# Where the attention mask of a fused state-space and attention kernel is applied: in the score matmuls, or, for the last of four groups, as products with the exponentials

## The chip, the cores and the metric

The kernel runs on one core of one Trainium2 chip. A core has five engines that run side by side, each with its own queue in program order: TensorE (PE in the profile; its weight loads are a row of their own, PEld), VectorE (DVE), ScalarE (ACT), GpSimd (POOL) and SyncE (SP), which here issues most of the DMAs. The metric is the device time of one execution in microseconds (us); lower is better.

## What is computed

The input is 32 sequences of 256 tokens with 256 channels. Each goes through a state-space layer (a projection, a short convolution, a layer norm, a recurrence over the tokens, a gate and an output projection) and then through two transformer layers with local attention and a feed-forward part; the input is added to the result. The part that matters here is the attention:

```python
# 8 heads of 64, windows of 128 tokens; each window looks at itself and at the one before
sim = jnp.einsum('bhwid,bhwjd->bhwij', bq, bk)
mask = (i < j) | (i > j + WINDOW) | (j == -1)
sim = jnp.where(mask, -jnp.finfo(sim.dtype).max, sim)
attn = jax.nn.softmax(sim, axis=-1)
out = jnp.einsum('bhwij,bhwjd->bhwid', attn, bv)
```

A query sees no later token, and of the window before only the tokens up to 128 back.

## The kernel before, in words

The 32 sequences are worked on in four groups of eight. The state-space part of a group is a scan over its 256 time steps, all eight sequences together (`group_scan`): VectorE does one recurrence step a token (L703), ScalarE scales the input rows (L693), TensorE reads the states out (L715), and SP loads the rows (L672). The scan of group 0 runs alone at the start. After that the scan of group g+1 runs beside the attention and feed-forward work of group g; when the last group has its turn, there is no scan left to run beside it.

The transformer work is a list of 64 turns, `seqs`: four groups, two layers, eight sequences. Each turn's work is cut into steps, and `stage(n, i, ...)` puts a step of turn n into stage i of eight (i may run on into the stages of later turns); a loop over the stages then emits the steps, in the order in which they were put into the list. So the attention of turn n stands beside the feed-forward steps of turns n-1 to n-3 and the projections of turn n+1. The order of the calls is the program's order; a scheduler may still move instructions within an engine's queue, unless `tc.keep_in_program_order` holds an instruction where it was written.

The steps of one turn that the change touches or that stand beside it:

- `project` (L962) projects queries, keys and values of the next turn, on TensorE, in stages 0, 1, 3 and 4; `rotated` then squares on ScalarE (L975), multiplies on VectorE (L978, L983), sums on VectorE (L988, L992), and on GpSimd adds (L986), takes a power (L994) and multiplies (L995).
- `turn` (L1001) transposes queries and keys on TensorE; ScalarE copies them (L1006).
- `scores(b, kw, i0, n)`: keys of window kw (0 or 1), pairs of heads i0 to i0+n. For each of two banks of PSUM, one matmul of the 128x128 identity (bf16) with the mask (bf16, repeated over the heads, 512 columns) writes the mask into the bank (L1161); the score matmuls (L1168) then add the scores to it. ScalarE takes the exponential of the whole bank into `pT` (L1177). The mask holds 0 where a key is seen and -32768 where not, so that the exponential there is 0. Scores of kw=1 stand in stage 2, of kw=0 in stages 3 (pairs 0 and 1) and 5 (pairs 2 and 3).
- `sums` (L1187) and `values` (L1206), both in stage 7, read `pT` on TensorE: the sums of the exponentials by head, and their products with the values. The reciprocal of the sums (L1195) goes through DRAM and comes back spread over the partitions; `divide` (L1230, VectorE, stage 4 of the next turn) multiplies it in, and `finish` (L1012 on TensorE, L1020 on VectorE, stage 6 of the next turn) does the output projection and adds it to the residual `res`.
- The feed-forward part: `normalise` (L1248, L1252 to L1258), `apply` (L1265), `spread` (L1278, L1280), `widen` (L1301 on TensorE, L1309 on ScalarE), `product` (L1317 on VectorE), `narrow` (L1329 on TensorE, L1340 on VectorE). In layer 1 `narrow` also adds the kernel's input on GpSimd (L1348) and issues the output's DMA.

All tiles in PSUM come from one pool of eight banks, and `pT` has six buffers, which is what one turn needs.

The tile of the mask is made once, at the set-up:

```python
mask_t = const.tile([P, 2 * W], BF, tag="mask_t", name="mask_t")
nc.gpsimd.memset(mask_t, 0.0)
nc.gpsimd.affine_select(
    out=mask_t[:, 0:W], in_=mask_t[:, 0:W], compare_op=ALU.is_ge, fill=MASKED_LOW,
    base=0, pattern=[[1, W]], channel_multiplier=-1,
)
```

The second half of it is filled in the same way with the sign turned round. The program holds a second path, `exact`, for inputs with large scales; it is not taken with these inputs and is the same in both kernels.

Of the kernel before, what the change touches and what calls it, by code (L numbers as in the profile page):

```python
# [11 lines left out]
BF = mybir.dt.bfloat16  # L12
I32 = mybir.dt.int32
AF = mybir.ActivationFunctionType
ALU = mybir.AluOpType
# [4 lines left out]
P = 128  # L20
# [18 lines left out]
W = 128  # L39
# [13 lines left out]
def bc(ap, axis, n):  # L53

    ap = ap.unsqueeze(axis)
    shape = list(ap.shape)
    shape[axis] = n
    return ap.broadcast_to(shape)
# [15 lines left out]
def kernel(  # L74
# [29 lines left out]
    nc = tc.nc  # L104
    B = xT.shape[2]
    L = wqkv.shape[1]
    NG = B // GB

    const = ctx.enter_context(tc.tile_pool(name="const", bufs=1))
# [53 lines left out]
    for j in range(NJ):  # L163
# [13 lines left out]
    mask_t = const.tile([P, 2 * W], BF, tag="mask_t", name="mask_t")  # L177
    ident_b = const.tile([P, P], BF, tag="ident_b", name="ident_b")
# [7 lines left out]
        out=mask_t[:, W : 2 * W], in_=mask_t[:, W : 2 * W], compare_op=ALU.is_ge,  # L186
        fill=MASKED_LOW, base=0, pattern=[[-1, W]], channel_multiplier=1,
    )

    head_cols = const.tile([P, 2, 32], FP, tag="head_cols", name="head_cols")  # L190
    nc.gpsimd.memset(head_cols, 0.0)
# [27 lines left out]
    def program(ctx, exact):  # L219
# [802 lines left out]
        if exact:  # L1022

            mask = rpool.tile([P, 2 * W], FP, tag="mask", name="mask")
# [102 lines left out]
        class Attention:  # L1127

            def __init__(self, l):
                self.l = l
                self.qkv, self.rot, self.p, self.o = {}, {}, {}, {}

            def project(self, b, w, a):
                if w == 0 and a == 2:
# [16 lines left out]
            def scores(self, b, kw, i0, n):  # L1153


                qT, kT, _ = self.qkv[b]
                nq = S - kw * W
                banks = []
                for r in range(2):
                    sc = ps_w.tile([P, n, nq], FP, tag="w", name="sc")  # L1160
                    nc.tensor.matmul(  # L1161
                        sc, ident_b, bc(mask_t[:, 0:nq], 1, n), start=True, stop=False
                    )
                    banks.append(sc)
                for i in range(n):
                    for r in range(2):
                        rows = slice(r * DH, (r + 1) * DH)
                        nc.tensor.matmul(  # L1168
                            banks[r][:, i, :],
                            kT[rows, i0 + i, kw * W : (kw + 1) * W],  # L1170
                            qT[rows, i0 + i, kw * W :],
                            start=False,
                            stop=(i == n - 1),
                        )
                for r in range(2):
                    p = aw.tile([P, n, nq], FP, tag="pT", name="pT", bufs=6)
                    nc.scalar.activation(p, banks[r], AF.Exp)  # L1177
                    for i in range(n):
                        self.p[b, kw, i0 + i, r] = p[:, i, :]

            def sums(self, b):

                rs = bank(ps_w, "w", "rs")[:, 0:S]
                for kw in range(NW):
                    for r in range(2):
                        for i in range(HEADS // 2):
                            nc.tensor.matmul(  # L1187
                                rs[32 * i : 32 * i + 32, kw * W :],
                                head_cols[:, r],
                                self.p[b, kw, i, r],  # L1190
                                start=(kw == 0 and r == 0),
                                stop=(kw == NW - 1 and r == 1),
                            )
                rinv = aw.tile([P, S], FP, tag="rinv", name="rinv", bufs=1)
                nc.vector.reciprocal(rinv, rs)  # L1195
                self.rinv = rinv
# [183 lines left out]
        seqs = [(g, l, b) for g in range(NG) for l in range(L) for b in range(GB)]  # L1380
        stages = {}

        def stage(n, i, what, *args):
            stages.setdefault(ST * n + i, []).append(partial(what, *args))

        def attend(n, at, b, nxt):

            stage(n, 0, at.turn, b, 1)
            stage(n, 3, at.scores, b, 0, 0, 2)
            stage(n, 2, at.scores, b, 1, 0, HEADS // 2)  # L1390
            stage(n, 5, at.scores, b, 0, 2, 2)
            stage(n, 7, at.sums, b)
            stage(n, 7, at.values, b)
            stage(n + 1, 0, at.put_inverse)
            stage(n + 1, 2, at.load_inverse)
            stage(n + 1, 4, at.divide, b)
            stage(n + 1, 6, at.finish, b)
            if nxt is not None:
                for w in range(NW):
                    for i, a in ((0, 2), (1, 0), (1, 1)):  # L1400
                        stage(n, 3 * w + i, nxt[0].project, nxt[1], w, a)
                stage(n, 6, nxt[0].turn, nxt[1], 0)
# [23 lines left out]
            if l == L - 1 and g < NG - 1:  # L1426
                stage(n + 6, 2, load_res, g + 1, b)

        ats = [Attention(l) for _, l, _ in seqs]

        for n, (g, l, b) in enumerate(seqs):
            nxt = (ats[n + 1], seqs[n + 1][2]) if n + 1 < len(seqs) else None
            attend(n, ats[n], b, nxt)
            feed(n, g, l, b)
# [24 lines left out]
        for t in range(max(stages) + 1):  # L1459
# [3 lines left out]
            g, r = divmod(t + 1 + group - reload, group)  # L1463
# [10 lines left out]
    with tc.If(fits > 0) as which:  # L1474
        with ExitStack() as es:
            program(es, False)
    with which.Else():
        with ExitStack() as es:
            program(es, True)
# [81 lines left out]
def _program(ins, out_shape):  # L1561
    import concourse.bacc as _bacc

    nc = _bacc.Bacc("TRN2", target_bir_lowering=False, num_devices=1)
    arrays, args = {}, []
    for name, a in ins.items():
        arrays[f"in_{name}_dram"] = a
        args.append(
            nc.dram_tensor(
                f"in_{name}_dram", a.shape, mybir.dt.from_np(a.dtype), kind="ExternalInput"  # L1570
            ).ap()
        )
    args.append(nc.dram_tensor("out_0_dram", out_shape, FP, kind="ExternalOutput").ap())
    with tile.TileContext(nc) as tc:
        kernel(tc, *args)
    return nc, arrays
# [11 lines left out]
```

## Time and profile before

| What | us |
|---|---|
| median of three runs (3755.57 to 3771.47) | 3759.6 |
| the profiled execution | 3750.8 |
| its span in the profile | 3748.7 |
| scan of group 0 alone, before the first score matmuls | 0 to 528 |
| one turn of the last group | 41.6 |
| last score matmuls of the last turn | about 3680 |

The profile's page gives, for each engine, its busy time, and then the span in 40 slices with the busy share in tenths. "Chain of waits" is the chain of work that ended last, followed back from the end. A timeline line gives the start, the duration, the engine, the line of the kernel, the operation, output and input tiles, shape and count; what stands in brackets at its end is the time for which the engine had been idle and what ended that. In a run of several instructions merged into one line ("x8") the duration runs from the first start to the last end, so that two lines of TensorE overlap a little. TensorE's float32 matmuls stand in the trace as two instructions each.

### The profile page before, as it was taken

The numbers are of one execution on the slowest core, as the hardware profiler recorded it, in microseconds if no ns is written. First come the engines' busy times: TensorE is split into PE (matmuls) and PEld (weight loads), VectorE is DVE, ScalarE is ACT, GpSimd is POOL, SyncE is SP. The second block draws the span as 40 slices with busy tenths as digits, with TensorE's granted clock in tenths as the row PEclk, the third lists the DMA queues.
The fourth block names the chain that finished last, engine by engine and source line by source line (L and its number), as shares of the span: only waits on it lengthen the run. The fifth ranks groups of instructions, "written<-read, shape, count | busy, mean of one in ns | idle before, by whom it ended". The sixth has DMA issues, their size and how long they took to land.

```text
span 3748.7 us, 57254 instructions
## 1 busy us (share of the span) xinstructions
PE 3601.1 (96%) x19900; PEld 2242.4 (60%) x19900; DVE 2669.6 (71%) x5177; ACT 2195.4 (59%) x3817; POOL 1834.9 (49%) x1776
## 2 busy tenths in 40 slices
PE   7999889999999999999999999999999999999998
PEld 4444335656656665665666665656666666666666
DVE  6888889888787787778777877777777444444443
ACT  4666656666666666666666665666666444444442
POOL 4433466545555565455455555645444444434441
PEclk9999999999999999999999999999999999999999
DMA  7777655445454545434444545444443211011101
GB/s 210 205 198 202 189 163 149 120 117 135 127 137 129 147 123 146 120 112 122 120 128 116 147 124 147 121 108 126 112 129 103 57 40 50 12 34 34 30 25 35
DMA packets 469214, 435.81 MB, mean 116 GB/s; under 512 B 228835, under 2 KB 308532, under 8 KB 468788
## 3 DMA queue, kind: packets, MB, share of 16 engines
q1 hardware_dynamic: 384466, 420.05, 40.1%
q10 hardware_dynamic: 84450, 12.01, 2.0%
q8 instruction: 160, 2.62, 0.3%
q14 instruction: 138, 1.13, 0.1%
HBM read 383.70 MB, written 46.66 MB: 115 GB/s over the span
## 4 chain that ended last, share of the span: by engine, by line
PE 62%; DVE 16%; POOL 7%; ACT 6%; DMA 5%; issue 3%; SPq 0%; ACTq 0%; DVEq 0%; POOLq 0%
PE ps_qkv L962 12%; PE pa L1301 12%; PE po_f L1329 7%; DVE h L703 6%; PE y L715 4%; PE ps_wo L1012 4%; DMA xrep<-xnd 4%; PE sc L1168 4%; PE ov L1206 3%; PE ps_out L793 2%; ACT xrep L693 2%; DVE acc L485 2%; PE tr_qk L1001 2%; PE ps_in L395 2%; POOL acc L474 2%
## 5 line engine op out<-in xcount | busy, mean ns | idle before, releaser
L703 DVE CUSTOM_DVE_ANT_0 h<-h,xrep,lim 128x512 f32<-128x512 f32 x1024 | 948.2, 926 | 269.2 <-ACT xrep L693 238.8
L693 ACT ACTIVATE xrep<-xrep,beta 128x512 f32<-128x512 f32 x960 | 674.1, 719 | 333.0 <-DMA xrep<-xnd 235.9
L962 PE MATMUL ps_qkv<-qkv,res 128*128 128x512 f32 x1536 | 727.1, 610 | 45.2 <-DVE ag L1317 30.1
L1301 PE MATMUL pa<-hT,w 128*128 128x256 f32 (+1 forms) x3072 | 688.3, 386 | 0.3 <-ACT oT L1213 0.3
L1301 PEld LDWEIGHTS pa<-hT,w 128*128 128x128 f32 (+1 forms) x3072 | 492.9, 178 | 183.7 <-issue 66.5
L962 PEld LDWEIGHTS ps_qkv<-qkv,res 128*128 128x128 f32 x1536 | 282.4, 194 | 335.4 <-issue 263.3
L986 POOL TENSOR_TENSOR rot<-rot,swp 128x512 f32<-128x512 f32 x256 | 336.5, 1314 | 293.0 <-DVE swp L983 239.2
L1258 POOL TENSOR_TENSOR rstd<-ve,neg_half 128x1 f32<-128x1 f32 x128 | 82.7, 646 | 792.9 <-DVE ve L1256 787.8
L994 POOL TENSOR_TENSOR rn<-ss,neg_half 128x8 f32<-128x8 f32 x256 | 460.3, 1798 | 14.8 <-DVE ss L992 5.0
L1329 PE MATMUL po_f<-ag,w 128*128 128x256 f32 (+1 forms) x1536 | 387.8, 394 | 4.8 <-DVE res L1340 1.1
L715 PE MATMUL y<-h,ly 128*32 128x512 f32 x2048 | 354.9, 612 | 12.9 <-DVE h L703 11.7
L1329 PEld LDWEIGHTS po_f<-ag,w 128*128 128x128 f32 (+1 forms) x1536 | 273.6, 190 | 112.9 <-issue 44.6
L1317 DVE SCALAR_TENSOR_TENSOR ag<-pa,b_sb,ag 128x256 f32<-128x256 f32 (+1 forms) x448 | 212.4, 474 | 166.5 <-ACT ag L1309 163.0
L975 ACT ACTIVATE sq<-ps_qkv 128x512 f32<-128x512 f32 x256 | 152.1, 596 | 270.5 <-PE ps_qkv L962 234.6
L995 POOL TENSOR_TENSOR rot<-rot,rn 128x512 f32<-128x512 f32 x256 | 298.6, 1166 | 20.1
L1309 ACT ACTIVATE ag<-pa,b_sb 128x256 f32<-128x256 f32 x320 | 150.4, 470 | 198.5 <-PE pa L1301 197.4
L1012 PE MATMUL ps_wo<-oT,wo 128*128 128x256 f32 x1024 | 231.6, 379 | 0.0
L485 DVE SCALAR_TENSOR_TENSOR acc<-xr,wc_sb,acc 128x256 f32<-128x256 f32 x384 | 192.7, 525 | 52.9 <-POOL acc L474 52.6
L1177 ACT ACTIVATE pT<-sc 128x512 f32<-128x512 f32 x384 | 208.5, 596 | 32.2 <-PE sc L1168 30.7
L1168 PE MATMUL sc<-qT,kT 64*128 64x128 f32 (+1 forms) x2048 | 221.5, 345 | 0.0
L978 DVE TENSOR_TENSOR rot<-ps_qkv,rc_sb 128x512 f32<-128x512 f32 x256 | 175.0, 683 | 56.5 <-ACT sq L975 55.9
L1012 PEld LDWEIGHTS ps_wo<-oT,wo 128*128 128x128 f32 x1024 | 194.5, 190 | 27.2 <-PE y L715 0.8
(150 smaller groups left out, 5534.7 us busy)
## 6 DMA issues: line engine op xcount, KB each, us to landing
xrep<-xnd SPq DMA_DIRECT2D x960, 256.0 KB
rb<-inv SPq DMA_DIRECT2D x128, 256.0 KB
xnd<-xn SPq DMA_DIRECT2D x64, 256.0 KB
qkv<-in_wqkv_dram SPq DMA_DIRECT2D x24, 512.0 KB
ahead<-xs_a SPq DMA_DIRECT2D x48, 256.0 KB
xp<-ahead SPq DMA_DIRECT2D x48, 256.0 KB
xd<-xnd SPq DMA_DIRECT2D x192, 64.0 KB
w<-in_w_dram SPq DMA_DIRECT2D x80, 128.0 KB
```

Of the source, the lines that this page charges most:

```text
L485: nc.vector.scalar_tensor_tensor(acc, xr[:, :, k : k + CH], wc_sb[:, ch, k : k + 1], acc, ALU.mult, ALU.add,)
L693: scaled = nc.scalar.activation(bx, ck[c].pop(("bx", t), bx), AF.Copy, scale=ck[c]["beta"][:, t : t + 1])
L703: nc.vector._custom_dve(TENSOR_ADD_SAT, out=h_new, in0=state["h"], in1=bx, s0=ck[c]["lim"][:, 0, t : t + 1], s1=ck[c]["lim"][:, 1, t : t + 1],
L715: nc.tensor.matmul(ck[c]["y", hb][32 * q : 32 * q + 32, :], ly[hb % 2][:, 32 * t : 32 * t + 32], ck[c].pop(("h", hb * TB + t)), start=(i = ...
L962: nc.tensor.matmul(ps, res[b][:, k, t0 : t0 + W], wt["qkv", a][:, k], start=(k == 0), stop=(k == KM - 1),)
L986: nc.gpsimd.tensor_add(rot, rot, swp)
L994: nc.gpsimd.tensor_tensor(rn, ss, neg_half, ALU.pow)
L995: nc.gpsimd.tensor_mul(rot, rot, bc(rn, 2, DH))
L1012: nc.tensor.matmul(po[:, d], wt["wo", 0][:, c, d * P : (d + 1) * P], oT[:, c, :], start=(c == 0), stop=(c == NC_ - 1),)
L1168: nc.tensor.matmul(banks[r][:, i, :], kT[rows, i0 + i, kw * W : (kw + 1) * W], qT[rows, i0 + i, kw * W :], start=False, stop=(i == n - 1),)
L1301: nc.tensor.matmul(pg if x else pa, wt["w1", m][:, k, x], self.h[:, k], start=(k == 0), stop=(k == KM - 1),)
L1329: nc.tensor.matmul(self.po[:, d], wt["w2", 0][r0 : r0 + n, m, d * P : (d + 1) * P], self.ag[m][r0 : r0 + n], start=(m == 0), stop=(m == le ...
```

## The change

For the last group (`apart`, true for g = NG - 1), `scores` leaves out the matmul that writes the mask, and each score matmul opens and closes its own accumulation. Instead a new step, `mask`, multiplies the exponentials in place by a tile of ones and zeros, `mask_1`, repeated over the heads. It does so on GpSimd for kw=1 (step in stage 3) and on VectorE for kw=0 (steps in stages 4 and 6), two products a step. `mask_1` is made once at the set-up from `mask_t`. The other three groups keep the matmul.

```diff
+    mask_1 = const.tile([P, 2 * W], BF, tag="mask_1", name="mask_1")
+    nc.gpsimd.tensor_scalar(mask_1, mask_t, -1.0, None, ALU.is_ge)
...
-            def __init__(self, l):
+            def __init__(self, g, l):
                 self.l = l
-                self.qkv, self.rot, self.p, self.o = {}, {}, {}, {}
+                self.apart = g == NG - 1
+                self.qkv, self.rot, self.p, self.ps, self.o = {}, {}, {}, {}, {}
...
                     sc = ps_w.tile([P, n, nq], FP, tag="w", name="sc")
-                    nc.tensor.matmul(
-                        sc, ident_b, bc(mask_t[:, 0:nq], 1, n), start=True, stop=False
-                    )
+                    if not self.apart:
+                        nc.tensor.matmul(
+                            sc, ident_b, bc(mask_t[:, 0:nq], 1, n), start=True, stop=False
+                        )
...
-                            start=False,
-                            stop=(i == n - 1),
+                            start=self.apart,
+                            stop=self.apart or i == n - 1,
...
                     nc.scalar.activation(p, banks[r], AF.Exp)
+                    self.ps[kw, i0, r] = p
...
+            def mask(self, kw, i0):
+
+                e = nc.gpsimd if kw else nc.vector
+                for r in range(2):
+                    p = self.ps.pop((kw, i0, r))
+                    n, nq = p.shape[1:]
+                    tc.keep_in_program_order(
+                        e.tensor_mul(p, p, bc(mask_1[:, 0:nq], 1, n))
+                    )
...
             stage(n, 5, at.scores, b, 0, 2, 2)
+            if at.apart:
+                for i, what in ((3, (1, 0)), (4, (0, 0)), (6, (0, 2))):
+                    stage(n, i, at.mask, *what)
             stage(n, 7, at.sums, b)
             stage(n, 7, at.values, b)
...
-        ats = [Attention(l) for _, l, _ in seqs]
+        ats = [Attention(g, l) for g, l, _ in seqs]
```

Beyond the added and removed instructions, the order in which the instructions of group 0's scan stand in the queues of all engines differs in places; those of groups 1 and 2 stand as before.

## The prediction

> **What bounds the kernel now.** I read the page's busy times first, then the slices, then the busy times by stretch, because the change touches one group of four.
>
> ```profile
> PE 3601.1 (96%) x19900; PEld 2242.4 (60%) x19900; DVE 2669.6 (71%) x5177; ACT 2195.4 (59%) x3817; POOL 1834.9 (49%) x1776
> ...
> PE   7999889999999999999999999999999999999998
> ...
> DVE  6888889888787787778777877777777444444443
> ```
>
> ```profile
> 3400.00:3500.00 100.00, 100.00 (x608) 68.25 (x606) 42.02 (x89) 46.74 (x77) 38.68 (x33) 1.00 0.18 47
> 3500.00:3600.00 100.00, 100.00 (x557) 66.06 (x554) 45.12 (x99) 48.07 (x78) 47.10 (x38) 1.00 0.09 22
> ```
>
> In the last quarter (columns of the second fence: length, then busy time of PE, PEld, DVE, ACT, POOL, the clock, DMA share) no scan runs any more: DVE falls to 4 tenths, POOL to 38 to 47%, and PE is busy for all of it at full clock. Of PE's few waits from 2850 us on, the sum is 3.5 us. So in this stage TensorE sets the pace, and a piece of its time taken out shortens the run, as long as nothing else makes it wait. The mask matmuls in that stretch wait for nothing either (120 of them from 2850 us on; the last group's 96 are among these):
>
> ```profile
> L1161 PE MATMUL sc<-mask_t,ident_b x120: 379/379/379, 2871.9 to 3678.9; 128*128 128x512 bf16 x120
> ```
>
> The 379 ns are a latency, not a price. The price is read where PE stands back to back, from the chain of waits and the PE timeline of one sequence:
>
> ```profile
> 3520.74 1.73 PE pa L1301 x8
> 3522.47 0.43 PE sc L1161 x2
> 3522.90 1.06 PE sc L1168 x8
> ```
>
> ```profile
> 3522.31 0.59 PE L1161 MATMUL sc<-mask_t,ident_b 128*128 128x512 bf16 x2
> 3522.83 1.13 PE L1168 MATMUL sc<-qT,kT 64*128 64x256 f32 x8
> ...
> 3529.18 1.04 PE L1001 MATMUL tr_qk<-ident,rot 128*128 128x128 f32 x8
> 3530.05 1.89 PE L1301 MATMUL pa<-hT,w 128*128 128x256 f32 x8
> 3531.88 1.51 PE L1187 MATMUL rs<-pT,head_cols 128*32 128x256 f32 x32
> ```
>
> By ends, a pair of mask matmuls takes 0.43 us; by starts, 0.52 us (3522.31 to 3522.83). A sequence of the last group takes 41.57 us (tp_h starts at 3496.33 and 3537.90) and holds three pairs.
>
> [...] L1168 uses 64 rows, L1161 all 128; the first weight load of L1168 indeed begins only with its first matmul. [...] The trace has 1.22 us for L1230 (1024 columns[...]) and 0.68 for L978 (512)[...]. [...] The trace shows who pays: L1348 takes 1.26 us alone and 2.12 beside L1230, while L1230 stays at 1.21 to 1.22.
>
> **The change part by part.** Sixteen sequences (two layers by eight) belong to the last group.
>
> *Removed.* 16 x 6 = 96 mask matmuls with their weight loads, 48 pairs. At 0.43 us a pair this is 20.6 us, all on the path. Ends of the unknown: 48 x 0.52 = 25.0 us if the start distance were the price; if the 0.19 us load of the first f32 weights of L1168 had so far been hidden by the masks, 48 x 0.24 = 11.5 us. I take 20.6, since the extra 0.09 of the start distance only reflects that a bf16 weight load is shorter[...]. Apart from the masks, the order of PE's instructions in the last group is the same in both programs, so nothing else moves there. That each score matmul now opens its own accumulation costs nothing: the count is the same.
>
> *Added on VectorE.* 64 products of 128x512, four a sequence, between 0.60 us (start distance of L978 and L983) and 0.69 us. Bound [...]above by 1.22 (as if it were 1024 columns). I take 0.65, 2.6 us a sequence on an engine with over 20 us idle.
> The first pair (heads block 0) stands behind L1230:
>
> ```profile
> 3515.83 1.22 DVE L1230 TENSOR_TENSOR oT<-oT,rb 128x1024 f32<-128x1024 f32 x1
> 3517.86 0.48 DVE L1317 SCALAR_TENSOR_TENSOR ag<-pa,b_sb,ag 128x256 f32<-128x256 f32 x1 [0.81 <-ACT ag L1309]
> ...
> 3529.38 0.69 DVE L1020 TENSOR_TENSOR res<-res,ps_wo 128x512 f32<-128x512 f32 x1 [1.70 <-PE ps_wo L1012]
> 3532.49 0.48 DVE L1317 SCALAR_TENSOR_TENSOR ag<-pa,b_sb,ag 128x256 f32<-128x256 f32 x1 [2.42 <-ACT ag L1309]
> ```
>
> It fills the 0.81 us gap and pushes L1317 by 0.5 us; the next operation, L978, waits until 3519.75 for ScalarE, and this ag is read by narrow a sequence later. Cost zero. The second pair is the one that matters: it stands behind L1020, which waits for ps_wo, and sums (L1187) waits for it. L1020 ends at 3530.07; two products take it to 3531.4. sums begins at 3531.88, reads the first product's output as its third head (0.18 us later) and the second's 0.54 us after its start, at 3532.4. Cover left: 1.0 us, and the first product has 1.3. Behind a waiting sums, PE would hold the values, widen and everything after. In the last sequence no turn stands between; L1020 ends at 3686.48, the pair at 3687.8, needed at 3687.95: still no wait.
>
> *Added on GpSimd.* 32 products, two a sequence, 1.04 (L995) to 1.27 us (L986), 2.3 us a pair. [...] In the queue they stand between the first and the second rotation:
>
> ```profile
> 3511.97 1.04 POOL L995 TENSOR_TENSOR rot<-rot,rn 128x512 f32<-128x512 f32 x1
> 3516.04 2.12 POOL L1348 TENSOR_TENSOR fo<-fo,xs 128x512 f32<-128x512 f32 x1 [3.02 <-DVE fo L1340]
> 3521.25 1.27 POOL L986 TENSOR_TENSOR rot<-rot,swp 128x512 f32<-128x512 f32 x1 [3.09 <-DVE swp L983]
> ```
>
> They need the exponentials that ScalarE finished at 3508.0, run in the 3.02 us gap, and end near 3515.3, sixteen us ahead of sums. L1348, which the VectorE pair now also slows, may end 1.2 us later, and so its output DMA; the square L975 that reuses the buffer may then slip by about a us. ScalarE and VectorE have over 1 us idle behind it before the second product. Cost zero.
>
> *Added once.* mask_1, one tensor_scalar of 128x256 on GpSimd in the set-up: 0.56 us by L474, inside the 1.08 us for which GpSimd waits at 3.6 us.
>
> *Moved.* The order of instructions on every engine changes in the first 500 us (group 0's scan), not in groups 1 and 2. On ScalarE the first tanh goes ahead of the last two parameter loads, which now hold it up:
>
> ```profile
> 20.50 0.72 ACT L493 ACTIVATE th<-acc 128x256 f32<-128x256 f32 x2 [9.86 <-DMA b_sb<-in_b_dram]
> ```
>
> SP issues the 768 KB w2 load about a hundred DMAs later, behind the first xq and xrep rows. Both should let the first scan step start 1 to 3 us sooner. In the later chunks single read-out, normalise and copy steps swap places; no duration tells what that costs. I bound the whole by -5 and +12 us (eight chunks by 1.5 us, about the length of two steps) and take -2.
>
> *Sum.* 20.6 + 2 = 22.6 us. The profiled execution took 3750.8 us around a span of 3748.7; it becomes 3728.2. The median of the runs shown is 3759.6, 8.8 above it; the same 22.6 us gives **3737.0 us**, 0.6% less.
>
> **The rivals.** (a) *The first group gives it back.* The re-ordering hits a stage that is bound by VectorE's chain of steps (432 of 527 us busy), where each lost us counts. For: the changes reach all eight chunks. Against: they are swaps of neighbours, and the start looks earlier. With +12 us: 3759.6 - 20.6 + 12 = 3751. (b) *Less is saved than the pair's length*, because the masks hid weight loads[...]: 11.5 us plus the 2 of the start, 3746. For: the first load of L1168 begins late. Against: it began no earlier behind the masks. (c) *The wait at sums takes over, and the kernel is slower.* Place: the second VectorE pair between L1020 and L1187. A pair has 2.35 us (3530.07 to 3532.4) and takes 1.3. Each us beyond is lost 16 times; the gain of 1.29 us a sequence is gone when the pair takes 3.65 us, 1.8 us a product. At 2.5 us a product it loses 2.65 us a sequence: 3759.6 - 22.6 + 42 = 3779. For: TensorE is in order and the cover short. Against: in this stage no VectorE operation of up to 512 columns takes over 0.7 us, except the reciprocal (1.76). That the masks stay on TensorE is excluded: the built order has 288 of 384 left.
>
> **How the numbers follow.** Forecast 0.60, own range 3728 to 3744; (a) 0.17, (b) 0.12, (c) 0.11. About 0.5% (18.8 us) is what a measurement can tell from no change: faster means under 3740.8. Of the forecast 0.55 lies there, of (a) and (b) 0.03 together; within 0.5%: 0.05 + 0.26 = 0.31; slower 0.11. The range, 3728 to 3756, takes in the forecast's ends, (b) and most of (a), and leaves out (c) and the tails.
>
> **What would show it.** Right: 24 mask matmuls from 2850 us on, PE still 100% busy from 3000 to 3600, 40.3 us a sequence, no PE wait for the products at L1187, products at 0.6 to 0.7 us (VectorE) and 1.0 to 1.3 us (GpSimd), first attention projection about 2 us sooner. Wrong: sums waiting for VectorE by over 0.3 us a sequence; scores L1168 taking over 1.2 us in the chain of waits; the first 500 us longer by more than 5.

## The result, and the profile after

| What, in us | before | after |
|---|---|---|
| median of five runs each | 3760.6 (3755.6 to 3771.5) | 3738.0 (3732.7 to 3741.3) |
| the profiled execution | 3750.8 | 3732.7 |
| its span in the profile | 3748.7 | 3730.9 |
| one turn of the last group | 41.57 | 40.28 |
| first residual addition (turn 0) | 597.3 | 595.0 |
| residual additions, turn 0 to turn 46 | 2433.2 | 2438.7 |
| residual additions, turn 46 to turn 63 | 681.5 | 660.8 |

The ratio of after to before is 0.9938, 95% interval 0.9923 to 0.9953: faster by 0.6%, or 22.6 us by the medians. The last three rows cut the profiled executions at the starts of the residual additions (L1020 before, L1023 after; lines move down by 3 to 17), one in each turn. The whole gain lies in the last row, 20.7 us. The row above it moves the other way by 5.4 us; the experiments show what that is worth.

The page of the changed kernel, its busy row and its slices:

```profile
PE 3587.1 (96%) x19804; PEld 2234.2 (60%) x19804; DVE 2719.1 (73%) x5241; ACT 2195.6 (59%) x3817; POOL 1872.6 (50%) x1809
...
PE   7999989999999999999999999999999999999998
...
DVE  6888889888887877787777777777777545555553
```

Busy time by stretch (the columns as before), and the mask matmuls that are left from 2850 us on:

```profile
3400.00:3500.00 100.00, 100.00 (x587) 66.74 (x580) 51.99 (x111) 49.50 (x82) 45.13 (x39) 1.00 0.17 42
3500.00:3600.00 100.00, 100.00 (x550) 68.75 (x548) 55.20 (x108) 48.68 (x77) 56.61 (x45) 1.00 0.09 25
```

```profile
L1167 PE MATMUL sc<-mask_t,ident_b x24: 379/379/379, 2875.1 to 3026.8; 128*128 128x512 bf16 x24
```

PE still has no idle time in the last quarter, with 24 masks in place of 120: the work became less and the bound stayed. DVE went from 42 and 45 to 52 and 55%. The chain of waits shows that nothing came in the masks' place; the feed-forward projection goes straight over into the scores, which take 1.06 us as before:

```profile
3508.81 1.73 PE pa L1318 x8
3510.54 1.06 PE sc L1174 x8
```

The timelines of VectorE, GpSimd and TensorE for one turn of layer 1:

```profile
3503.90 1.36 DVE L1247 TENSOR_TENSOR oT<-oT,rb 128x1024 f32<-128x1024 f32 x1
3505.18 2.35 DVE L1195 TENSOR_TENSOR pT<-pT,mask 128x512 f32<-128x512 f32 x2
3507.45 0.47 DVE L1334 SCALAR_TENSOR_TENSOR ag<-pa,b_sb,ag 128x256 f32<-128x256 f32 x1
...
3517.02 0.69 DVE L1023 TENSOR_TENSOR res<-res,ps_wo 128x512 f32<-128x512 f32 x1 [1.26 <-PE ps_wo L1015]
3517.62 1.29 DVE L1195 TENSOR_TENSOR pT<-pT,mask 128x512 f32<-128x512 f32 x2
```

```profile
3500.90 1.04 POOL L998 TENSOR_TENSOR rot<-rot,rn 128x512 f32<-128x512 f32 x1
3501.90 2.27 POOL L1195 TENSOR_TENSOR pT<-pT,mask 128x512 f32<-128x512 f32 x2
3504.13 2.25 POOL L1365 TENSOR_TENSOR fo<-fo,xs 128x512 f32<-128x512 f32 x1
3509.33 1.28 POOL L989 TENSOR_TENSOR rot<-rot,swp 128x512 f32<-128x512 f32 x1 [2.95 <-DVE swp L986]
```

```profile
3516.82 1.04 PE L1004 MATMUL tr_qk<-ident,rot 128*128 128x128 f32 x8
3517.69 1.89 PE L1318 MATMUL pa<-hT,w 128*128 128x256 f32 x8
3519.51 1.51 PE L1204 MATMUL rs<-pT,head_cols 128*32 128x256 f32 x32
```

The second pair ends at 3518.91, before sums (L1204) begins at 3519.51, and sums takes 1.51 us, as long as before the change. The first pair takes 2.35 us instead of 1.29, next to L1365 on GpSimd; that is so in eight of the 16 turns, in those where L1365 runs beside it. All products together (durations are shortest, median and longest):

```profile
L1195 DVE TENSOR_TENSOR pT<-pT,mask x64: 677/684/1759, 3062.1 to 3669.5; 128x512 f32<-128x512 f32 x64
L1195 POOL TENSOR_TENSOR pT<-pT,mask x32: 1150/1157/1164, 3058.9 to 3653.6; 128x512 f32<-128x512 f32 x32
```

### The profile page after: what moved, and what is told of

It is laid out like the page before. It is cut to its first block, busy times and chain, and to the rows that moved or that the text cites. A ratio compares the mean times of both kernels' runs of the same rounds, so it can differ in the third digit from the quotient of the medians.

```text
span 3730.9 us, 57179 instructions
## 1 busy us (share of the span) xinstructions
PE 3587.1 (96%) x19804; PEld 2234.2 (60%) x19804; DVE 2719.1 (73%) x5241; ACT 2195.6 (59%) x3817; POOL 1872.6 (50%) x1809
## 4 chain that ended last, share of the span: by engine, by line
PE 63%; DVE 16%; POOL 6%; DMA 6%; ACT 5%; issue 3%; SPq 0%; ACTq 0%; DVEq 0%; POOLq 0%
PE ps_qkv L965 13%; PE pa L1318 12%; PE po_f L1346 7%; DVE h L706 6%; PE ps_wo L1015 5%; PE y L718 4%; PE sc L1174 4%; DMA xrep<-xnd 4%; PE ov L1223 3%; PE ps_out L796 2%; ACT xrep L696 2%; PE tr_qk L1004 2%; DVE acc L488 2%; PE ps_in L398 2%; PE rs L1204 2%
## 5 line engine op out<-in xcount | busy, mean ns | idle before, releaser
L706 DVE CUSTOM_DVE_ANT_0 h<-h,xrep,lim 128x512 f32<-128x512 f32 x1024 | 946.7, 925 | 261.6 <-ACT xrep L696 230.5
L989 POOL TENSOR_TENSOR rot<-rot,swp 128x512 f32<-128x512 f32 x256 | 335.9, 1312 | 269.0 <-DVE swp L986 220.2
L1334 DVE SCALAR_TENSOR_TENSOR ag<-pa,b_sb,ag 128x256 f32<-128x256 f32 (+1 forms) x448 | 211.9, 473 | 139.4 <-ACT ag L1326 135.7
L978 ACT ACTIVATE sq<-ps_qkv 128x512 f32<-128x512 f32 x256 | 152.1, 596 | 271.1 <-PE ps_qkv L965 231.7
L488 DVE SCALAR_TENSOR_TENSOR acc<-xr,wc_sb,acc 128x256 f32<-128x256 f32 x384 | 191.8, 522 | 54.7 <-POOL acc L477 53.6
L981 DVE TENSOR_TENSOR rot<-ps_qkv,rc_sb 128x512 f32<-128x512 f32 x256 | 174.6, 682 | 46.3 <-ACT sq L978 46.1
```

The costliest lines, as they stand in the source:

```text
L488: nc.vector.scalar_tensor_tensor(acc, xr[:, :, k : k + CH], wc_sb[:, ch, k : k + 1], acc, ALU.mult, ALU.add,)
L706: nc.vector._custom_dve(TENSOR_ADD_SAT, out=h_new, in0=state["h"], in1=bx, s0=ck[c]["lim"][:, 0, t : t + 1], s1=ck[c]["lim"][:, 1, t : t + 1],
L989: nc.gpsimd.tensor_add(rot, rot, swp)
```

## The experiments

Two theories stood at the start. The prediction's: TensorE sets the pace of the last group, a pair of masks is worth its 0.43 us, the products are hidden, and the new order of the first group is worth little. Against it: the new order costs something (rival a; the profile's 5.4 us speak for it), the products take something back (rival c), or the price of a pair is another (rival b).

All kernels first, by the same cuts as above. The last two columns are of one profiled execution each. The ratio is to the kernel before, run beside each; "turn" is one of the last group.

| Kernel | median | ratio, 95% interval | turn | turn 0 to 46 | turn 46 to 63 |
|---|---|---|---|---|---|
| before | 3758 to 3762 | 1 | 41.57 | 2433.2 | 681.5 |
| changed | 3738.0 | 0.9938 (0.9923 to 0.9953) | 40.28 | 2438.7 | 660.8 |
| e1, set-up and order alone | 3756.2 | 0.9993 (0.9982 to 1.0004) | 41.57 | 2432.4 | 681.5 |
| e2, no products | 3737.2 | 0.9944 (0.9927 to 0.9961) | 40.28 | 2437.5 | 660.8 |
| e3, second pair three times | 3755.2, one run | none | 41.39 | 2437.4 | 679.0 |
| e4, masks twice | 3784.8 | 1.0075 (1.0055 to 1.0095) | 42.87 | 2435.6 | 702.2 |
| e5, second pair twice | 3741.1 | 0.9950 (0.9934 to 0.9966) | 40.73 | 2437.5 | 668.8 |
| e6, products in all groups | 3798.1 | 1.0100 (1.0084 to 1.0115) | 40.28 | 2492.2 | 660.8 |
| e7, all products on GpSimd | 3733.8 | 0.9925 (0.9911 to 0.9940) | 40.28 | 2438.5 | 660.8 |
| e8, GpSimd's pair in all groups | 3763.5 | 1.0014 (1.0007 to 1.0021) | 40.28 | 2460.7 | 660.7 |
| e9, e8 without its products there | 3722.4 | 0.9884 (0.9867 to 0.9901) | 40.28 | 2429.3 | 660.7 |
| e10, window 1 masked twice there | 3774.3 | 1.0027 (1.0015 to 1.0038) | 41.57 | 2450.8 | 681.5 |
| e11, products from turn 40 on | 3734.3 | 0.9927 (0.9913 to 0.9941) | 40.28 | 2435.8 | 660.8 |
| e12, e8 with one-input products | 3765.1 | 1.0011 (1.0000 to 1.0023) | 40.28 | 2465.9 | 660.7 |

One thing that blurs the column of turns 0 to 46 can be read from the traces. Their records of TensorE's granted clock have two values, full and half. Between turns 0 and 46 the stretches at half clock last 34.1 us in all in before, 38.6 in the changed kernel and 21.2 in e1; from 2850 to 3650 us there are none. Take from the column TensorE's idle time in it (64.0, 68.0 and 68.7 us) and half the length of these stretches, and 2352.1, 2351.3 and 2353.2 us are left; in e2 to e5 and in e7 it is 2351.9 to 2353.4. These kernels do the same work there, and what is left agrees within some 2 us, where the column itself spreads over 6. That a stretch at half clock costs half of its length is an estimate from the two values of the record; that the remainders then meet speaks for it. The sections below call this the remainder.

### e1: set-up and order alone

```diff
+    mask_1 = const.tile([P, 2 * W], BF, tag="mask_1", name="mask_1")
+    nc.gpsimd.tensor_scalar(mask_1, mask_t, -1.0, None, ALU.is_ge)
```

> The kernel before with mask_1 made in the set-up and used nowhere; its instructions stand on every engine in the order of the changed kernel, the masks stay matmuls in all groups. It measures the prediction's part 'moved' alone. Theory of the prediction: the start is 2 us earlier and nothing else differs, so 2 us less than before (within 4 of it either way, which is inside the spread). Theory that the new order costs something in groups 0 and 1 (the trace of the changed kernel drifts by +5.4 us against before between turns 0 and 14): about 3 us more than before, and the drift shows here again at the same turns. If the drift is a difference between any two executions, it shows at other turns or not at all.

Measured: 0.9993, that is -2.6 us with an interval of -6.8 to +1.5. A cost of 3 us lies outside it, and so do the 12 us of rival (a). The drift did come back in part (from turn 0 to turn 8 this execution lost 4.1 us on before), but so it did in e4, by 4.4, and e4's order is that of before. The 0-to-46 column spreads over 6 us among kernels that do the same there in the same order (2432.4 in e1, 2438.7 in the changed kernel). Of the 5.4 us in the table of the result, 4.0 are idle time of TensorE and some 2 the clock, and e4, in the order of before, idles for 68.2 us, as long as the changed kernel does. So they are a difference between two executions, in which before was a quick one; they are not the change's.

### e2: no products

```diff
-            if at.apart:
+            if False:
                 for i, what in ((3, (1, 0)), (4, (0, 0)), (6, (0, 2))):
                     stage(n, i, at.mask, *what)
```

> The changed kernel without the products: the last group has no mask at all, and its attention sees every token of its two windows. The order of all other instructions is that of the changed kernel. It measures what the products cost. Theory of the prediction: they cost nothing, so the time is that of the changed kernel, 3738, within 2 us (in the last turn alone sums waited 0.3 us for one). Rival: the products take part of the gain back, through waits at sums or through a later output; 16 turns by a us would give 3722. A turn of the last group stays at 40.28 us in the first case.

Measured: 3737.2 and a turn of 40.28, the changed kernel's. From turn 46 to 63 it needs 660.75 us, as the changed kernel does. The 96 products, 64 x 0.68 and 32 x 1.16 us by the medians above, 81 us of engine time, cost nothing that shows.

### e4: masks twice

```diff
+                self.twice = g == NG - 1
...
                     nc.tensor.matmul(
                         sc, ident_b, bc(mask_t[:, 0:nq], 1, n), start=True, stop=False
                     )
+                    if self.twice:
+                        nc.tensor.matmul(
+                            sc, ident_b, bc(mask_t[:, 0:nq], 1, n), start=False, stop=False
+                        )
```

> The kernel before with each mask matmul of the last group issued twice into the same bank (the mask is added twice, which leaves the exponentials as they are), same order. It measures the price of a mask matmul from the other side. If a pair costs its distance by ends, 0.43 us: 48 x 0.43 = 20.6 us more than before, a turn of 42.86 us. If it cost its distance by starts, 0.52 us: 25 more. If part of a mask is cover for the first weight load of the scores[...], the second mask still costs its whole 0.43 while taking one away saved less: then adding costs more than the 1.29 us a turn that taking away gave.

Measured: a turn of 42.87, 1.30 more than before; taking the masks away gave 1.29. Turns 46 to 63 took 20.7 us more, the same size as the gain with the sign turned. The price of a pair is 0.43 us from both sides, so no part of a mask was cover for the first weight load of the scores, and rival (b) is out. (The medians are 26.8 apart; of the profiled execution's excess 10 us lay ahead of turn 46, 8 of them already ahead of the first residual addition, where the two programs are the same; TensorE's clock stands at half there for 77.7 us, and for 58.0 in before.)

### e5: the second VectorE pair twice

```diff
-                    tc.keep_in_program_order(
-                        e.tensor_mul(p, p, bc(mask_1[:, 0:nq], 1, n))
-                    )
+                    for _ in range(2 if i0 else 1):
+                        tc.keep_in_program_order(
+                            e.tensor_mul(p, p, bc(mask_1[:, 0:nq], 1, n))
+                        )
```

> The changed kernel with the two VectorE products of the second pair done twice each (ones and zeros, so the second time changes nothing). It tests the prediction's cover at sums: the pair has 2.35 us from the end of the residual addition and takes 1.29; doubled it takes 2.6. Theory: sums waits about 0.25 us a turn, 4 us in all, so about 3742. If the cover is longer than thought: 3738, no wait. If it is shorter, the wait is over 0.5 us a turn, 3746 or more.

The cover is the time by which the pair could end later before sums has to wait for it. Measured: 0.45 us more a turn, 8 us from turn 46 to 63, and 3 us by the medians, which the spread of the early stages blurs. The direction is the expected one; the size lies between the 0.25 that was expected and the 0.5 that would have meant a short cover, and the expectation had set the four products at 2.6 us where they take 2.74. Timeline of e5, with TensorE's weight loads (PEld), beside sums:

```profile
3319.34 0.69 DVE L1023 TENSOR_TENSOR res<-res,ps_wo 128x512 f32<-128x512 f32 x1 [0.66 <-PE ps_wo L1015]
3319.94 2.74 DVE L1196 TENSOR_TENSOR pT<-pT,mask 128x512 f32<-128x512 f32 x4
3321.83 0.58 PEld L1205 LDWEIGHTS rs<-pT,head_cols 128*32 128x32 f32 x12 [0.33 <-issue]
3321.83 1.96 PE L1205 MATMUL rs<-pT,head_cols 128*32 128x256 f32 x32
3322.73 0.79 PEld L1205 LDWEIGHTS rs<-pT,head_cols 128*32 128x32 f32 x20 [0.33 <-DVE pT L1196]
```

From the start of the residual addition the pair now ends after 3.34 us (3322.68) and in the changed kernel after 1.89 us (3518.91), 1.45 later; 0.45 of it is seen. The cover was therefore 1.0 us, as the prediction had it. Two things are to be seen in the lines. The wait lies inside sums, between its first 12 weight loads and the other 20, so that the merged PE line grows from 1.51 to 1.96 us. And PE counts as busy through it: from 3400 to 3500 us e5 has

```profile
3400.00:3500.00 100.00, 100.00 (x604) 67.13 (x604) 55.33 (x115) 46.26 (x77) 40.48 (x37) 1.00 0.19 47
```

100.00 of 100, though each turn stands still for 0.45 us. So a stall inside a run of matmuls is counted as busy here, and the busy share of the weight loads doesn't show it either (67.13 us here, 66.74 in the changed kernel). The turn's period and the weight loads' idle time were what told.

### e3: the second pair three times

```diff
-                    for _ in range(2 if i0 else 1):
+                    for _ in range(3 if i0 else 1):
```

> The changed kernel with the two products of the second VectorE pair done three times each, 4.0 us in all, more than the 3.65 at which the prediction's rival (c) puts the end of the gain. Doubling the pair cost 0.45 us a turn. With the order unchanged the wait would be 0.45 + 1.36 = 1.8 us a turn and a turn 42.1 us, over the 41.57 of the kernel before. The scheduler, however, puts nine matmuls of the values ahead of the last two of the sums here, about 1.6 us: if these cover, the wait is 0.2 to 0.3 us, and a turn 40.5 us.

Measured: a turn of 41.39, 1.11 us over the changed kernel's and 0.18 under before's. Neither expectation holds. The scheduler moved nine matmuls of the values up, ahead of the last ten of the sums and not of the last two, and they cover part of the wait only: in the timeline from 3284 us on, the weight loads stand idle for 0.41 us where sums is cut in two and for 0.38 us at its second part. The six products took 4.46 us with a gate product (L1335) between them. That is longer than the 3.65 us at which rival (c) turns the gain into a loss, and 0.18 us of the gain is still there. Whether 3.65 us is right for the unchanged order isn't shown; no run with so long a pair has that order. The time from turn 46 to 63, 679.0, is still below before's 681.5, by 2.5 us.

### e7: all products of the last group on GpSimd

```diff
-                e = nc.gpsimd if kw else nc.vector
+                e = nc.gpsimd
```

> The changed kernel with all six products of a turn of the last group on GpSimd, same order. It tests the same cover for the other engine: the second pair stands behind GpSimd's last multiplication of the rotation, which ends at 3316.03 in the changed kernel; at 1.15 us each the products end at 3317.2 and 3318.3, and sums needs them at 3318.3 and 3318.7. Theory: no wait or up to 0.3 us a turn, 3738 to 3743. Rival: the products (7 us a turn) push the rotations, and TensorE waits at the transposes, over 0.5 us a turn, 3746 or more.

Measured: the turn is 40.28 again and the ratio's interval overlaps the changed kernel's, so the two are the same. Seven us of products a turn fit into GpSimd's gaps too; in its timeline the second pair ends at 3526.66, just behind the rotation that it follows:

```profile
3523.38 1.04 POOL L998 TENSOR_TENSOR rot<-rot,rn 128x512 f32<-128x512 f32 x1
3524.38 2.28 POOL L1195 TENSOR_TENSOR pT<-pT,mask 128x512 f32<-128x512 f32 x2
```

Which engine takes the products doesn't matter in this stage: both have room.

### e8, e9, e10: a pair beside a running scan

e8 masks window 1 by GpSimd's products in all four groups; e9 is e8 without these products in groups 0 to 2; e10 is before with window 1's mask matmul issued twice there. In e8, against the changed kernel:

```diff
+                apart = self.apart or kw == 1
...
-                    if not self.apart:
+                    if not apart:
...
-            if at.apart:
-                for i, what in ((3, (1, 0)), (4, (0, 0)), (6, (0, 2))):
+            stage(n, 3, at.mask, 1, 0)
+            if at.apart:
+                for i, what in ((4, (0, 0)), (6, (0, 2))):
                     stage(n, i, at.mask, *what)
```

> The changed kernel with the GpSimd pair (keys of window 1) as products in all four groups, so that groups 0 to 2 lose one of their three pairs of mask matmuls; the VectorE pairs stay in the last group alone. It asks whether the saving of 0.43 us a pair holds beside a running scan, where TensorE is 96 to 98% busy. If TensorE sets the pace there too and GpSimd's products are hidden: 48 pairs x 0.43 = 20.6 us less than the changed kernel, 3717. If the scan's steps on VectorE set it, and GpSimd's two-input operations stretch them (0.81 us alone, 1.1 to 1.3 beside GpSimd in the kernel before): no gain or a loss, 3738 or more.

In e9, against e8:

```diff
-            stage(n, 3, at.mask, 1, 0)
             if at.apart:
-                for i, what in ((4, (0, 0)), (6, (0, 2))):
+                for i, what in ((3, (1, 0)), (4, (0, 0)), (6, (0, 2))):
```

> The kernel with GpSimd's pair as products in all groups, without its products in groups 0 to 2, where window 1 is then not masked at all. Its instructions stand in the same order as there. It splits the 25 us by which that kernel was slower than the changed one. If TensorE sets the pace beside the scan and GpSimd's products alone spoiled it: 48 x 0.43 = 20.6 us less than the changed kernel, 3717. If TensorE's time is worth nothing beside the scan (its waits grow by what is taken out) and the rest is the products: the changed kernel's 3738. If it is the order of the instructions, which the scheduler moves in places: 3750 or more here too.

In e10, against e4:

```diff
-                self.twice = g == NG - 1
+                self.twice = g < NG - 1
...
-                    if self.twice:
+                    if self.twice and kw == 1:
```

> The kernel before with the mask matmul of window 1 issued twice in groups 0 to 2 (48 pairs more; the exponentials stay as they are). The price of a pair beside the scan, from the other side; the order of the instructions moves in places here too. If TensorE sets the pace there: 20.6 us more than before, 3779. If the scan's chain on VectorE and ScalarE does: within 5 us of before, 3760.

Measured: e8 is slower than before. e9 is faster than the changed kernel by 0.0054 of 3760, 20 us (the two intervals leave 8 either way), or 15.6 by the medians; e10 is 10 us slower than before (6 to 14). So TensorE's time is worth something beside the scan too. How much, the traces tell better. The remainder, as defined above, is 2330 us in e8, 2332 in e9 and 2371 in e10, against 2351 to 2353 in the kernels that issue each mask matmul once there: 48 pairs are 19 to 23 us of TensorE's work there, as in the last group (20.6). What of this the whole time shows hangs on the two terms that were taken off, idle time and clock. In e9's profiled execution, the slowest of its four, the clock stood at half for 53.6 us, and from turn 0 to 46 only about 8 us were gained on the like of e2 and e5; in e10 TensorE idled for 60.9 us instead of 64.0 to 68.2, and 16 us were lost on before and e4. Whether these two terms moved by chance or through the edit, one trace of each kernel can't tell.

What spoils e8 is the products: with the same order of all other instructions it is 41 us slower than e9 by the medians, 31 from turn 0 to 46. There TensorE idles for 96.1 us instead of 70.5, and its clock stands at half for 69.2 us instead of 53.6, by the estimate 8 us more. So the products cost 26 us in waits and some 8 in clock. By stretch, e9 and then e8 (length, busy time of PE, PEld, DVE, ACT and POOL, clock, DMA share, GB/s):

```profile
600.00:2850.00 2250.00, 2179.47 (x12509) 1377.70 (x12502) 1773.53 (x3399) 1427.56 (x2492) 1223.82 (x1132) 0.99 0.48 127
600.00:2850.00 2250.00, 2153.92 (x12345) 1360.66 (x12338) 1779.64 (x3356) 1405.35 (x2457) 1314.36 (x1197) 0.98 0.47 125
```

The groups of instructions on VectorE between 600 and 2850 us, e9 and then e8:

```profile
L706 DVE CUSTOM_DVE_ANT_0 h<-h,xrep,lim 128x512 f32<-128x512 f32 x692 | 644.4, 931 | 225.5 <-ACT xrep L696 202.7 <-DVE h L706 6.2 <-PE y L718 4.4
...
L488 DVE SCALAR_TENSOR_TENSOR acc<-xr,wc_sb,acc 128x256 f32<-128x256 f32 x246 | 117.3, 520 | 31.7 <-POOL acc L477 31.6
```

```profile
L706 DVE CUSTOM_DVE_ANT_0 h<-h,xrep,lim 128x512 f32<-128x512 f32 x681 | 659.4, 968 | 207.7 <-ACT xrep L696 187.1 <-DVE h L706 5.2 <-PE y L718 2.3
...
L488 DVE SCALAR_TENSOR_TENSOR acc<-xr,wc_sb,acc 128x256 f32<-128x256 f32 x246 | 120.8, 537 | 61.4 <-POOL acc L477 61.2
```

With the products, a recurrence step (L706) takes 37 ns more, 25 us over 681 steps, and the filter (L488) waits 61 us for its first tap on GpSimd (L477) instead of 32. TensorE gets it through the gate (L1335), for which the masks that are left now wait 26.3 us instead of 3.3, by PE's waits in the same stretch.

### e12: one input instead of two

Against e8:

```diff
-                    tc.keep_in_program_order(
-                        e.tensor_mul(p, p, bc(mask_1[:, 0:nq], 1, n))
-                    )
+                    if self.apart:
+                        i = e.tensor_mul(p, p, bc(mask_1[:, 0:nq], 1, n))
+                    else:
+                        i = e.tensor_scalar(p, p, 1.0, None, ALU.mult)
+                    tc.keep_in_program_order(i)
```

> The kernel with GpSimd's pair as products in all groups, in the same order, but in groups 0 to 2 GpSimd multiplies the exponentials by the number 1 (one input from SBUF) instead of by the tile of ones and zeros (two inputs), so that window 1 is not masked there. It tells apart how 96 products on GpSimd cost 41 us beside the scan. If they cost through their place in GpSimd's queue (the first filter tap behind them comes later): about as much, 3755 to 3764. If they cost by stretching the recurrence steps on VectorE[...]: most of it is gone, 3725 to 3735.

That a one-input form would stretch the steps less was an estimate: in the profile before, a step beside the one-input L474 alone (128x256) took 0.80 us in the mean of 27, and one beside the two-input L574 alone (128x512) 1.16 us in the mean of 34, 1.76 at most; the shapes differ too.

Measured: as slow as e8, with as much idle time of TensorE (95.8 us from turn 0 to 46). The steps L706 went back in part (946 ns), and the wait of L488 for GpSimd grew to 72.5 us. That refutes stretched steps as the whole cause and speaks for the place in GpSimd's queue. It doesn't settle the shares, because the one-input form was the longer one, 1.49 us by the median against 1.17 in e8.

### e6: products in all groups

```diff
-                self.apart = g == NG - 1
+                self.apart = True
```

> The changed kernel with all three pairs as products in all four groups; no mask matmul is left. If TensorE sets the pace everywhere and the products are hidden: 144 pairs x 0.43 = 62 us less than the changed kernel, 3676. If VectorE's queue is the limit beside the scan (79% busy between 900 and 1900 us), where the 192 products add 192 x 0.68 = 130 us to it and sums stands behind them: TensorE waits at sums and the time is the changed kernel's or longer, 3738 to 3800.

Measured: 3798, 60 us more than the changed kernel although no mask matmul is left. PE's waits between 600 and 2850 us in e6 (total, times, longest) begin with

```profile
PE rs L1204 <- DVE pT L1195: 100.8, 39, 6.8
```

This is rival (c)'s mechanism: sums waits for the VectorE pair, which stands behind steps of the scan in VectorE's queue. From turn 0 to 46 TensorE idles for 128.8 us instead of the changed kernel's 68.0, and its clock stands at half for 119.5 us instead of 38.6, by the estimate 40 us more. The two together, 101 us, outweigh the 62 us that the masks were worth; the column grows by 53.5, so some 15 us more went elsewhere, and waits inside sums that count as busy, as in e5, are one possible place. In the last group of the very same run the same products cost nothing (660.8 us).

### e11: products from turn 40 on

```diff
-                self.apart = g == NG - 1
+                self.apart = g == NG - 1 or (g == NG - 2 and l == L - 1)
```

> The changed kernel with the products from turn 40 on (group 2's second layer and group 3), where the traces show no more waits for the scan and the gain of a pair at its full 0.43 us from turn 41 or so. Eight turns more at 1.29 us: 10 us less than the changed kernel, 3728, if the last steps of the scan are done by then. If the scan's end still counts in half of these turns, or the products delay it: 3733 to 3738.

Measured: 3734, inside the range of the second expectation, and not to be told from the changed kernel (the intervals overlap). Against it the profiled execution gained 5.9 us between the residual additions of turns 41 and 46, 1.3 in each of the last four steps, after it had lost 2.9 between those of turns 38 and 41, where the last steps of the scan still run and sums waited 4.3 us in three turns for VectorE. No kernel tried that keeps the whole mask is measurably better than the changed one.

## Why the prediction was right, step by step

- **Removed masks**: right. 20.6 us were forecast; 20.7 lie between turns 46 and 63, 48 pairs at 0.43. The price by ends was the right one of the two that the trace offered; e4 confirms it by adding. The 0.09 us by which the price by starts is longer are as much as two weight loads differ in the profile before, 98 ns for the masks' in bf16 and 186 for the scores' in float32. That the masks hid no part of the scores' first load was an estimate, until e4.
- **Products on VectorE**: their price was right (0.68 us measured, 0.65 taken), and so was the cover of the second pair, 1.0 us (e5). In the last turn it waited after all, by 0.33 us on one weight load; the prediction had 0.15 us in hand there.
- **First pair**: mis-sized. The prediction took the pair for 1.3 us and read from L1348 beside L1230 that GpSimd alone pays there. In eight of the turns the pair takes 2.35 us, one product of it 1.76. From the start of the division (L1247, L1230 before) to that of the gate product behind it (L1334, L1317 before) it is 3.55 us for 2.03, 1.5 us later where 0.5 were forecast. Nobody waited for it, as forecast: VectorE then stands idle for 2.82 us ahead of its third L1334, and e2 is no faster.
- **Products on GpSimd**: right, 1.157 us each; they end 15.3 us ahead of sums. L1365 takes 2.25 us, little more than it mostly did before (2.12), and not the 1.2 us more that the prediction allowed for. As forecast, the output's DMA comes later: from 2900 us on the square L978 waits for it 9.9 us in eight times, before 4.1 in three; none of it reaches TensorE.
- **Set-up**: mask_1 took 0.87 us where 0.56 was forecast; GpSimd is still idle for 0.24 us behind it. Nothing lost.
- **Moved**: the size fits, and isn't shown. -2 us was taken and e1 has -2.6, with zero inside its interval. The start itself moved as forecast. The first tanh starts at 17.3 to 17.9 us in the eleven kernels that begin in the new order and at 20.5 to 21.4 in the three that begin as before does; in the changed kernel:

```profile
17.39 0.42 ACT L496 ACTIVATE th<-acc 128x256 f32<-128x256 f32 x1 [6.84 <-DMA flg_sb<-in_f_ln_g_dram]
```

  The first recurrence step follows at 55.3 to 60.8 us in the eleven and at 57.3 to 63.9 in the three, 3.1 us earlier by the means; these ranges overlap, so that single traces (55.26 for 57.34 in the two compared here) can't carry the size.
- **Sum**: 22.6 us forecast and 22.6 between the medians. That they meet to the tenth is luck: the interval is 18 to 29 us, and only the 20.7 are pinned down.
- **Rivals**: (a) is refuted by e1 and (b) by e4. (c) named a true mechanism: beside the scan e6 shows it 100.8 us strong. In the last group even the pair done three times left 0.18 us a turn of the gain (e3).
- **What would show it**: PE's 100% was a weak sign, as e5 teaches; the period of a turn was the strong one.

## What to carry to other kernels

Where one engine had no gap, its work was worth its back-to-back length (0.43 us a pair, whether taken away or added), and moving it paid where the receiving engine's queue had room at that very place: the same products were free in the last group (660.8 us from turn 46 to 63 with them and without) and cost more than the matmuls they replaced beside the scan (60 us over the changed kernel in e6, 25.5 in e8), so such a choice belongs to a stage and not to a kernel. Price a moved step by the distance from the instruction ahead of it in its new queue to its first reader, and test that cover by doubling the step. Judge by a period of the repeating work: it repeated to 0.01 us here, where whole executions differ by some 10 us, with the clock as one part of it, and the busy shares hid a stall of 0.45 us a turn (e5).

## What the runs showed of the hardware

**Where L1247, L1365 and a product overlapped, the instruction that started later took longer, on GpSimd as on VectorE.** The prediction read from one pair of instructions that GpSimd pays and VectorE doesn't. In the timelines of the changed kernel, L1365 starts at 3504.13 while L1247 runs until 3505.26, and takes 2.25 us instead of 1.26, ending at 3506.38; the first product starts at 3505.18 and takes 1.76 instead of 0.68, ending at 3506.94. If L1365 stood until L1247 was done, it ran 1.1 us from there; if the product then stood until L1365 was done, it ran 0.56 us. Both are about their lengths alone. That the later one stands until the earlier one is done is an estimate from these times; no run shows the cause. Not every overlap does it: in the same kernel L989 takes 1.27 us by the median beside L981, L991 and L995 on VectorE (105 times) and 1.27 alone (32). By the estimate, the durations of 2.25 and 1.76 us hold waits that no idle time shows.

**TensorE's granted clock fell to half in short stretches while the scan ran, and for longer in all where TensorE stood idle for longer.** Between turns 0 and 46 it was at half for 21 to 42 us in the kernels in which TensorE idled for 61 to 72 us (e9, with 53.6, apart), for 69.2 and 83.4 us in e8 and e12 (idle for 96), and for 119.5 us in e6 (idle for 128.8). In e8 each of the 16 stretches between 600 and 2850 us begins less than 9 us after the start of an idle time of over 2.2 us. No experiment changed the idle time alone, so that the one brings about the other is not shown. The clock is also a part of the spread of whole executions: of the 74 of before beside the experiments, the 19 with a mean clock of 0.984 took 3764.5 us on average, the 12 with 0.987 took 3757.5.

**A one-input product on GpSimd was not shorter than one with two inputs**: 1.49 us (128x512, times a number, e12) against 1.17 us (times a tile, e8), by medians.
